# Spreading inverse key norms over a head's rows: products into PSUM or transfers on chip

## The chip, the cores and the metric

The kernel runs on one core of one Trainium2 chip. The time is the device time of one execution in microseconds (us). The engines are TensorE (PE, with its weight loads as PEld), VectorE (DVE), ScalarE (ACT), GpSimd (POOL) and SyncE (SP), which here issues all transfers.

## What is computed

A "macaron" block on 2048 tokens of 128 features: half a step of a six-layer local-attention network, a linear-attention block, and half a step of the same six-layer network again. Everything is float32. The twelve local-attention layers take nearly all of the time. One of them, cut to what matters:

```python
qkv = shift_tokens(x) @ Wqkv                 # 16 heads of 64
q = l2norm(q) * qs ; k = l2norm(k) * ksc     # norm over a head's 64 features
q = q*cos*scale + rotate_half(q)*sin*scale   # rotary, with a growing scale
k = k*cos/scale + rotate_half(k)*sin/scale
sim = 8 * (q . k)  over the own window of 32 tokens and the one before, masked
out = softmax(sim) @ v ; x = out @ Wo + x
x = ffn(shift_tokens(x)) + x                 # layer norm, gated GELU, 341 wide
```

Rotary turns a head's two halves of 32 features into each other and keeps tokens apart, so the inverse norm of a key, one number for each head and token, can be multiplied onto the rotated key.

## The kernel before

Activations lie with features on the 128 partitions and tokens along the free dimension. A layer goes through 8 chunks of 256 tokens; a chunk goes through 4 steps. In a chunk, queries and keys are made in two halves of eight heads (`g2` = 0, 1). In the tile `d["k", g2]` (named abk in the profile, 128 x 2 x 2 x 256) the 128 partitions are 4 groups of 32 feature rows, each group belonging to one head; `i` (0 or 1) picks which four of the eight heads, and `u` which half of a head's features.

The steps that matter, in the order in which data passes through them:

- `project` (L286): TensorE products into PSUM tiles p. VectorE multiplies p with the rotary tables (prod, L295), GpSimd adds the two products (abq and abk, L301). ScalarE squares p (L307), GpSimd adds the two halves of the squares (L321).
- `square_sums` (L329): TensorE sums the squares over each head's rows into the PSUM tile ss. Rows 64 to 127 of ss hold the keys' sums: row 64 + 32i + 4 g2 + j is head j of the four with `i` in half `g2`.
- `norms` (L400 to L408): VectorE and ScalarE make the inverse norms rn (128 rows x 256 tokens, float32) from ss.
- `query_norms` (L416, L422) takes the queries' inverse norms to the scale of the softmax.
- `scale_keys` (L430, L436): the step that changes. Two TensorE products with the 0/1 matrix `sel_r` spread the four rows of rn over their heads' 32 feature rows each, into two PSUM tiles r. VectorE multiplies each onto its half of abk. Then `gather` (L393) issues four transfers that put the keys head by head into hk.
- `earlier_keys` (L450, L451) fills hk's first 32 columns from the chunk before. `similarities` (L466, L476, L488, L489), `exponentials` (L501), `normalised` (L511, L513), `transposed` (L526, L532), `values` (L553, L560, L562) and `output` (L569, L578) are the attention, one step of eight heads and 128 tokens at a time. `values_windows` (L365 to L368) issues the transfers of the value windows vw, `gather` with "q" (L387) those of the queries hq.
- `feed_forward` (L603, L609, L614, L622), for 512 tokens, is spread over the steps of two chunks.

All transfers go through SyncE's one queue, in the order in which they are issued. PSUM has a ring of five tiles ("small") which nearly every TensorE step takes from in turn, two tiles for the scores and one for ss.

The order of all work is written out by hand: the table POS gives each step of each function (a generator, cut at its `yield`) a place (step, position) relative to its chunk. The plan is sorted by step and position, and each engine carries out its own instructions in that order. Before, the first half's `scale_keys` has both parts at (-3, 69) and (-3, 70), the second half's at (-1, 119) and (-1, 136), and the three parts of `norms` are at (-4, 38), (-4, 43) and (-4, 63).

Of the kernel before, what the change touches and what calls it, by code (L numbers as in the profile page):

```python
# [8 lines left out]
F32 = mybir.dt.float32  # L9
BF16 = mybir.dt.bfloat16  # L10
AF = mybir.ActivationFunctionType
ALU = mybir.AluOpType
# [3 lines left out]
P = 128  # L16
# [6 lines left out]
CH = 512  # L23
NCH = N // CH
AC = 256
# [5 lines left out]
HID = 512  # L31
LN_EPS = 1e-5
POS = {
    "tabq": [(-10, 141)],
    "tabk": [(-9, 110)],
    "ss": [(-7, 142)],
    "vwin": [(1, 8)],
    "gq0": [(-5, 13)],
    "gq1": [(-3, 49)],
    "e0": [(0, 76)],  # L40
    "e1": [(0, 77)],
    "nrm": [(1, 10)],
    "qn": [(-2, 106)],
    "ek": [(-1, 73)],
    "proj": [(-9, 135), (-8, 33), (-8, 36), (-8, 37), (-8, 39), (-8, 101)],
    "vproj": [(-2, 24), (-2, 71)],
    "norms": [(-4, 38), (-4, 43), (-4, 63)],
    "sk0": [(-3, 69), (-3, 70)],
    "sk1": [(-1, 119), (-1, 136)],
    "te": [(2, 46), (2, 47)],  # L50
    "av": [(2, 132), (2, 177), (2, 178)],
    "out": [(4, 92), (4, 115)],
    "sim": [(0, 50), (0, 53), (0, 54)],
    "ff": [(11, 99), (12, 30), (12, 130), (13, 21), (13, 94), (14, 139), (15, 124), (15, 149),
        (16, 12), (17, 87), (17, 122), (18, 14), (18, 45), (18, 52), (18, 184), (21, 107),
        (21, 167)],
    "ff2": [(12, 15), (12, 80), (13, 95), (14, 58), (14, 60), (14, 79), (15, 91), (16, 40),
        (16, 58), (16, 147), (16, 182), (16, 187), (16, 191), (17, 34), (17, 111), (17, 121),
        (17, 157)],
    "ff3": [(10, 171), (10, 172), (10, 174), (10, 181), (10, 183), (10, 184), (11, 25), (11, 35),  # L60
        (11, 57), (11, 68), (11, 86), (11, 100), (11, 103), (11, 104), (11, 146), (11, 170),
        (11, 170)],
    "start0": [(-16, 180), (-14, 143), (-13, 66), (-11, 67), (-10, 109), (-10, 185)],
    "start1": [(-10, 65), (-9, 134), (-8, 96), (-8, 148), (-6, 20), (-6, 26)],
    "start2": [(-7, 2), (-7, 117), (-6, 6), (-6, 48), (-4, 74), (-4, 176)],
    "start3": [(-6, 28), (-4, 32), (-4, 44), (-4, 75), (-4, 98), (-4, 188)],
    "sums0": [(-9, 105), (-8, 5), (-8, 88), (-8, 123), (-8, 134), (-7, 102), (-7, 118), (-6, 27)],
    "sums1": [(-1, 137), (-1, 145), (0, 56), (0, 114), (1, 116), (1, 133), (2, 154), (2, 172)],
    "sums2": [(1, 189), (2, 173), (2, 178), (2, 192), (3, 144), (3, 153), (4, 125), (4, 126)],
    "sums3": [(3, 179), (4, 11), (4, 19), (4, 42), (4, 82), (4, 83), (4, 84), (4, 128)],  # L70
    "kv": [(5, 1)],
    "outs0": [(5, 3), (5, 4), (5, 7), (5, 9), (5, 22), (5, 85), (6, 18), (6, 113), (6, 164),
        (7, 17), (7, 90), (7, 129), (7, 163), (7, 190)],
    "outs1": [(6, 61), (11, 78), (12, 131), (13, 120), (13, 127), (13, 140), (13, 160), (14, 59),
        (14, 186), (15, 29), (15, 41), (15, 112), (15, 138), (15, 165)],
    "outs2": [(5, 23), (13, 51), (13, 62), (13, 169), (14, 31), (14, 55), (14, 166), (14, 168),
        (15, 44), (15, 64), (15, 159), (16, 150), (16, 158), (17, 97)],
    "outs3": [(5, 175), (15, 93), (16, 16), (16, 81), (16, 151), (16, 160), (16, 161), (17, 72),
        (17, 89), (17, 108), (17, 152), (17, 156), (17, 162), (18, 155)],
}  # L80
EXP_LN = "natural_log_exp_and_others"

# [11 lines left out]
def kernel(ctx: ExitStack, tc: tile.TileContext, a: dict, out: bass.AP):  # L94
    nc = tc.nc

    const = ctx.enter_context(tc.tile_pool(name="const", bufs=1))
    work = ctx.enter_context(tc.tile_pool(name="work", bufs=2))
# [4 lines left out]
    def small(name):  # L103
        return ps_small.tile([P, CH], F32, tag="small", name=name)

    def keep(shape, name, dtype=F32, src=None):
        t = const.tile(shape, dtype, name=name)
        if src is not None:
            dims = "abc"[: len(shape) - 1]
            flat = t.rearrange(f"p {' '.join(dims)} -> p ({' '.join(dims)})") if len(dims) > 1 else t  # L110
            if dtype == F32:
                nc.sync.dma_start(flat, src)
            else:
                nc.sync.dma_start(t, src)
        return t

    def load_qk(l, g):
        w = const.tile([P, 4, P], F32, tag=f"wqk{g}", name=f"wqk{g}_{l}")
        nc.sync.dma_start(
            w,  # L120
            a["Wqk"][l % DEPTH].rearrange("p (g f) -> p g f", g=4)[:, g, :]
            .rearrange("p (u f) -> p u f", u=4),
        )
        return w
# [25 lines left out]
    def load_x(f):  # L150
        nc.sync.dma_start(xo[:, f * CH : (f + 1) * CH], a["xT"][:, f * CH : (f + 1) * CH])

    load_x(0)
    sq_consts = keep([P, 5, P], "sq_consts", src=a["squares"].rearrange("p a b -> p (a b)"))
    ident, hmask, rot_m = (sq_consts[:, i, :] for i in range(3))
    sel_r = sq_consts[:, 3:5, :]
    wqk = [load_qk(0, g) for g in range(4)]
    rot = keep([P, 2, 2, AC], "rot", src=a["rot"])
    qks = keep([P, DEPTH, 2, 2], "qks", src=a["qks"])
# [108 lines left out]
    def chunk(l, c):  # L268
        return chunks.setdefault((l, c), {"nm": f"{l}_{c}"})
# [154 lines left out]

    def scale_keys(l, c, g2):
        d = chunk(l, c)
        rs = [small(f"r_{d['nm']}_{2 * g2 + i}") for i in range(2)]
        for i in range(2):
            rows = slice(64 + 32 * i, 96 + 32 * i)
            nc.tensor.matmul(  # L430
                rs[i][:, 0:AC], sel_r[rows, g2, :], d["rn"][rows, :], start=True, stop=True
            )
        yield
        for i in range(2):
            k = d["k", g2][:, :, i, :]
            nc.vector.tensor_tensor(  # L436
                k, k, rs[i][:, 0:AC].unsqueeze(1).to_broadcast([P, 2, AC]), ALU.mult
            )
        gather(l, c, "k", g2)

    def earlier_keys(l, c):
# [392 lines left out]
def _shape_constants():  # L834

    import ml_dtypes
    import numpy as np

    freqs = np.arange(0, DH, 2, dtype=np.float64)
    inv = 1.0 / 10000.0 ** (freqs / DH)  # L840
    base = (freqs + 0.4 * DH) / (1.4 * DH)
    t = np.arange(AC, dtype=np.float64)[None, :]
    ang = inv[:, None] * t

    scale = base[:, None] ** ((t - AC // 2) / (WIN // 2))
    cos, sin = np.cos(ang), np.sin(ang)
    rot = np.stack(
        [
            np.stack([8.0 * cos * scale, 8.0 * sin * scale], 1),
            np.stack([cos / scale, sin / scale], 1),  # L850
        ],
        1,
    )

    rot *= 2.0**9
    rot = np.tile(rot.reshape(32, -1), (4, 1)).astype(np.float32)

    back = base ** (AC / (WIN // 2))
    c, s = np.diag(back * np.cos(AC * inv)), np.diag(back * np.sin(AC * inv))
    one = np.block([[c, -s], [s, c]]).reshape(2, 32, 2, 32).transpose(1, 0, 3, 2).reshape(64, 64)  # L860
    rot_m = np.kron(np.eye(2), one)


    i, j = np.arange(WIN)[:, None], np.arange(SK)[None, :]
    near = (j >= i) & (j <= i + WIN)
    off = np.stack([~near, near & (j < WIN)], 1)
    band = np.zeros((2, 2 * WIN, 2, SK), np.float32)
    band[:, :WIN] = np.where(off, -(2.0**100), 0.0)
    band = band.reshape(P, 2, SK).astype(ml_dtypes.bfloat16)
    ident_b = np.tile(np.eye(2 * WIN, WIN), (2, 1)).astype(ml_dtypes.bfloat16)  # L870
    r = np.arange(P)
    sel_r = [r[:, None] % 32 == 4 * i + r[None, :] // 32 for i in range(2)]
    squares = np.stack(
        [r[:, None] == r[None, :], r[:, None] // 8 == r[None, :] // 8, rot_m, *sel_r], 1
    ).astype(np.float32)

    sel = np.zeros((P, 3, 32), np.float32)
    for i in range(2):
        sel[r, i, 4 * i + r // 32] = 2.0**18
    for h in range(HEADS):  # L880
        sel[32 * (h // 2 % 2) + 4 * (h // 8) + 2 * (h // 4 % 2) + h % 2, 2, h] = 1.0
    return {
        "rot": rot,
        "band": band,
        "ident_b": ident_b,
        "squares": squares,
        "sel": sel,
    }


def _laid_out(i):

    import numpy as np

    g = {k: np.asarray(v) for k, v in i.items()}
    a = _shape_constants()
    a["xT"] = g["L0_attn_x"][0].T
    w = g["L0_ffn_Wqkv"]
# [47 lines left out]
```

## Time and profile before

| | |
|---|---|
| median of 3 runs | 3537.21 us (3536.9 to 3539.05) |
| profiled execution | 3536.21 us, of which the profile's span is 3534.4 us |
| mean granted TensorE clock | 0.981 |
| TensorE busy | 3392.8 us (96%) |
| VectorE busy | 2553.6 us (72%) |
| ScalarE busy | 2738.4 us (77%) |
| GpSimd busy | 2092.2 us (59%) |
| L430 on TensorE (r) | 768 records, 145.1 us, mean 429 ns |
| L436 on VectorE (keys times r) | 384 instructions, 246.7 us, mean 684 ns |
| transfers | 396.13 MB, mean 112 GB/s |

A busy time is the union of an engine's instructions. Lines such as L436 are lines of the kernel's file, with the tile written, an arrow and the tiles read. A float32 product on TensorE shows as several records. In a list of idle times, the name behind the arrow is what ended the wait.

### The profile page before, as it was taken

How to read it: one execution, taken by the hardware profiler on the slowest of the kernel's cores; microseconds unless marked ns; L12 is line 12 of the kernel's file. 1: busy time of each engine (PE TensorE's matmuls, PEld its weight loads, DVE VectorE, ACT ScalarE, POOL GpSimd, SP SyncE). 2: the span in 40 equal slices, each digit the busy share in tenths (PEclk: the TensorE clock that was granted, in tenths of full speed). 3: DMA queues.
4: the chain of work that ended last, by engine and by line, in shares of the span. 5: the costliest groups of instructions: out<-in, count | busy, mean ns of one | idle time of the engine just before them, and what ended most of it. 6: DMA issues, size and time to landing. Idle time of an engine off the chain costs nothing.

```text
span 3534.4 us, 154488 instructions
## 1 busy us (share of the span) xinstructions
PE 3392.8 (96%) x64856; PEld 2346.8 (66%) x64856; DVE 2553.6 (72%) x5116; ACT 2738.4 (77%) x8805; POOL 2092.2 (59%) x2195
## 2 busy tenths in 40 slices
PE   7999999999999999999678999999999999999998
PEld 4776776666776677666335777767667666776674
DVE  5777777777777777775336777777777777777774
ACT  4788788878878878887446787888788788788877
POOL 6766666666666566563136666666666666666661
PEclk9999999999999999999788999999999999999999
DMA  4554544444545455444003544545545454544552
GB/s 123 127 127 119 118 120 117 117 122 120 124 115 126 115 122 131 107 115 104 12 12 83 125 123 123 119 114 126 120 122 120 112 127 119 118 121 117 117 123 61
DMA packets 295921, 396.13 MB, mean 112 GB/s; under 512 B 45501, under 2 KB 160953, under 8 KB 295225
## 3 DMA queue, kind: packets, MB, share of 16 engines
q1 hardware_dynamic: 295224, 386.25, 45.3%
q8 instruction: 510, 8.36, 1.0%
q14 instruction: 187, 1.52, 0.1%
HBM read 34.27 MB, written 1.05 MB: 10 GB/s over the span
## 4 chain that ended last, share of the span: by engine, by line
PE 35%; ACT 8%; DVE 6%; issue 1%; POOL 0%; DMA 0%; ACTq 0%; SPq 0%; POOLq 0%; DVEq 0%
PE p L286 7%; ACT e L501 5%; PE av L553 4%; PE y L569 4%; PE pv L345 4%; DVE prod L295 3%; PE sim L476 3%; PE pf L603 2%; PE yf L622 2%; PE te L526 2%; ACT L607 1%; PE r L430 1%; PE ss L329 1%; PE sim L466 1%; DVE eT L532 1%
## 5 line engine op out<-in xcount | busy, mean ns | idle before, releaser
L501 ACT ACTIVATE e<-sim,st,rq 128x64 f32<-128x64 f32 x3072 | 1194.5, 410 | 292.3 <-DVE st L489 288.9
L295 DVE TENSOR_TENSOR prod<-p,tab 128x1024 f32<-128x1024 f32 x768 | 922.3, 1212 | 130.9 <-ACT sq L307 96.1
L513 POOL TENSOR_TENSOR e<-e,st 128x512 f32<-128x512 f32 x384 | 400.5, 1043 | 724.9 <-DVE st L511 697.6
L286 PE MATMUL p<-xa,wqk 128*128 128x256 f32 x3072 | 773.5, 395 | 18.3 <-ACT sq L307 6.3
L301 POOL TENSOR_TENSOR abq<-prod 128x512 f32<-128x512 f32 x384 | 490.2, 1276 | 297.5 <-DVE prod L295 252.9
L501 ACT ACTIVATION_READ_ACCUMULATOR e<-sim,st,rq 128x1 f32 x3072 | 647.9, 211 | 0.0
L307 ACT ACTIVATE sq<-p 128x512 f32<-128x512 f32 x768 | 438.8, 602 | 248.0 <-PE ss L329 101.4
L286 PEld LDWEIGHTS p<-xa,wqk 128*128 128x128 f32 x3072 | 558.2, 191 | 106.5 <-ACT sq L307 9.6
L301 POOL TENSOR_TENSOR abk<-prod 128x512 f32<-128x512 f32 x384 | 487.2, 1269 | 166.6 <-DVE prod L295 89.5
L321 POOL TENSOR_TENSOR sq<-sq 128x256 f32<-128x256 f32 x768 | 546.9, 734 | 0.0
L553 PEld LDWEIGHTS av<-eT,vw 64*64 64x64 f32 x18432 | 401.7, 135 | 171.3 <-DVE st L489 48.0
L553 PE MATMUL av<-eT,vw 64*64 64x32 f32 x18432 | 446.8, 221 | 3.4 <-issue 1.1
L345 PE MATMUL pv<-wv,xa 128*128 128x512 f32 x768 | 413.4, 620 | 19.4 <-ACT gate L609 18.7
L569 PE MATMUL y<-oT,wo 128*128 128x128 f32 x3072 | 395.1, 282 | 0.2 <-DVE oT L562 0.2
L553 PE MATMUL av<-eT,v 64*64 64x32 f32 x6144 | 390.9, 219 | 0.0
L569 PEld LDWEIGHTS y<-oT,wo 128*128 128x128 f32 x3072 | 359.0, 192 | 19.4 <-issue 1.7
L488 DVE TENSOR_REDUCE sim<-sim 128x4 f32<-128x256 f32 x768 | 325.4, 424 | 14.1 <-PE sim L476 14.0
L476 PE MATMUL sim<-hk,hq 64*32 64x64 f32 x24576 | 332.9, 222 | 0.0
L526 PEld LDWEIGHTS te<-sq_consts,e 128*128 128x128 f32 x1536 | 188.5, 141 | 209.4 <-issue 151.6
L553 PEld LDWEIGHTS av<-eT,v 64*64 64x64 f32 x6144 | 325.6, 135 | 0.0
L476 PEld LDWEIGHTS sim<-hk,hq 64*32 64x32 f32 x24576 | 305.6, 105 | 0.2
L603 PE MATMUL pf<-xc,w 128*128 128x512 f32 (+1 forms) x576 | 290.4, 629 | 11.9 <-POOL xc L591 7.5
(141 smaller groups left out, 4549.6 us busy)
## 6 DMA issues: line engine op xcount, KB each, us to landing
hq<-abq SPq DMA_DIRECT2D x384, 256.0 KB
hk<-abk SPq DMA_DIRECT2D x768, 128.0 KB
vw<-v SPq DMA_DIRECT2D x768, 128.0 KB
vw<-v SPq DMA_DIRECT2D x744, 64.0 KB
wqk<-in_Wqk SPq DMA_DIRECT2D x48, 256.0 KB
wv<-in_Wv SPq DMA_DIRECT2D x24, 256.0 KB
wo<-in_Wo SPq DMA_DIRECT2D x12, 512.0 KB
w<-in_W SPq DMA_DIRECT2D x12, 341.0 KB
```

The costliest lines, as they stand in the source:

```text
L286: nc.tensor.matmul(both[s][:, u, :], wqk[g][:, 2 * s + u, :], xs, start=True, stop=True)
L295: nc.vector.tensor_tensor(prod, both[s].unsqueeze(2).to_broadcast([P, 2, 2, AC]), tabs[l, s].rearrange("p (u v) t -> p u v t", u=2), ALU.mult,
L301: nc.gpsimd.tensor_tensor(d["qk"[s], g // 2][:, :, g % 2, :], prod[:, 0], prod[:, 1], ALU.add)
L307: nc.scalar.activation(sq, both[s], AF.Square)
L321: nc.gpsimd.tensor_tensor(sq[:, 0, :], sq[:, 0, :], sq[:, 1, :], ALU.add)
L345: nc.tensor.matmul(ps, xa[:, ti * P : (ti + 1) * P], wv[j], start=True, stop=True)
L476: nc.tensor.matmul(sims[par][WIN * b : WIN * b + WIN, i, :], d["hq"][rows, 4 * h8 + i, at : at + WIN], d["hk"][rows, 4 * h8 + i, at : at + ...
L501: nc.scalar.activation(e[:, i, par, :], d["sims", step][par][:, i, :], AF.Exp, bias=st8[:, 0, i, par : par + 1], scale=rq[:, i, par : par ...
L513: nc.gpsimd.tensor_tensor(ef, ef, st8[:, 1].rearrange("p i r -> p (i r)").unsqueeze(2).to_broadcast([P, 8, SK]), ALU.mult,)
L553: nc.tensor.matmul(av[u][r : r + 64, m, WIN * b : WIN * b + WIN], d["vs", t][u][b][:, at : at + DH], d["eT", step][64 * u : 64 * u + 64, i ...
L569: nc.tensor.matmul(y[:, 0:P], wo[:, i, :], d["oT", t].rearrange("p h u m q -> p (h u m) q")[:, i, :], start=(i == 0), stop=(i == 7),)
L603: nc.tensor.matmul(ps[s][:r], w1[:, s, j * P : j * P + r], x, start=True, stop=True)
```

## The change

`scale_keys` no longer uses TensorE and PSUM. For each half and each `i`, SyncE issues a transfer within SBUF that reads the four rows of rn and writes each of them 32 times, into 128 rows of a new SBUF tile rk (128 x 2 x 256, two buffers). VectorE then multiplies the whole half, both `i`, in one instruction of 1024 elements per partition. The matrix `sel_r` goes, and with it 128 KB of the first load of constants. Then `gather` follows as before.

The table POS is new in nearly all its entries. Those that the text speaks of:

| step | before | after |
|---|---|---|
| norms | (-4, 38), (-4, 43), (-4, 63) | (-4, 37), (-4, 67), (-4, 110) |
| sk0 | (-3, 69), (-3, 70) | (-4, 111), (-3, 73) |
| sk1 | (-1, 119), (-1, 136) | (-4, 141), (-1, 140) |
| vwin | (1, 8) | (1, 62) |
| gq0, gq1 | (-5, 13), (-3, 49) | (-6, 129), (-3, 56) |
| proj, last part | (-8, 101) | (-8, 55) |

```diff
-    sq_consts = keep([P, 5, P], "sq_consts", src=a["squares"].rearrange("p a b -> p (a b)"))
+    sq_consts = keep([P, 3, P], "sq_consts", src=a["squares"].rearrange("p a b -> p (a b)"))
     ident, hmask, rot_m = (sq_consts[:, i, :] for i in range(3))
-    sel_r = sq_consts[:, 3:5, :]
...
     def scale_keys(l, c, g2):
         d = chunk(l, c)
-        rs = [small(f"r_{d['nm']}_{2 * g2 + i}") for i in range(2)]
+        r = work.tile([P, 2, AC], F32, tag="rk", name=f"rk_{d['nm']}_{g2}", bufs=2)
         for i in range(2):
-            rows = slice(64 + 32 * i, 96 + 32 * i)
-            nc.tensor.matmul(
-                rs[i][:, 0:AC], sel_r[rows, g2, :], d["rn"][rows, :], start=True, stop=True
-            )
-        yield
-        for i in range(2):
-            k = d["k", g2][:, :, i, :]
-            nc.vector.tensor_tensor(
-                k, k, rs[i][:, 0:AC].unsqueeze(1).to_broadcast([P, 2, AC]), ALU.mult
-            )
+            row = 64 + 32 * i + 4 * g2
+            nc.sync.dma_start(
+                r[:, i, :],
+                d["rn"][row : row + 4, :].unsqueeze(1).to_broadcast([4, 32, AC]),
+            )
+        yield
+        k = d["k", g2].rearrange("p u i t -> p u (i t)")
+        nc.vector.tensor_tensor(
+            k, k, r.rearrange("p i t -> p (i t)").unsqueeze(1).to_broadcast([P, 2, CH]),
+            ALU.mult,
+        )
         gather(l, c, "k", g2)
```

## The prediction

> **What bounds the kernel now.** I read the page first (busy time by engine, then the slices), then a table by stage of one repeat in the middle of the layers, then the order of events on TensorE, VectorE and SyncE inside that repeat.
>
> ```profile
> span 3534.4 us, 154488 instructions
> ...
> PE 3392.8 (96%) x64856; PEld 2346.8 (66%) x64856; DVE 2553.6 (72%) x5116; ACT 2738.4 (77%) x8805; POOL 2092.2 (59%) x2195
> ...
> q1 hardware_dynamic: 295224, 386.25, 45.3%
> ```
>
> TensorE is busy for 96% of the span; the DMA engines carry 45.3% on one queue. The stage table (length, then busy us of each engine) covers one repeat, two chunks of 256 tokens:
>
> ```profile
> 1000.00:1068.06 68.06, 67.66 (x1366) 47.71 (x1363) 51.94 (x105) 55.42 (x183) 45.17 (x50) 1.00 0.47 118
> ```
>
> Of 68.06 us TensorE is busy 67.66, VectorE 51.94, ScalarE 55.42, GpSimd 45.17, at the full granted clock. The twelve layers are 48 such repeats, 3267 of 3534 us. So what leaves TensorE's order shortens the kernel, as long as the others keep feeding it. In order of time on TensorE, the product that goes:
>
> ```profile
> 1007.24 0.84 PE L476 MATMUL sim<-hk,hq 64*32 64x64 f32 x64
> 1008.01 0.70 PE L430 MATMUL r<-rn,sq_consts 32*128 32x256 f32 x4
> 1008.64 1.99 PE L603 MATMUL pf<-xc,w 128*128 128x512 f32 x4
> ```
>
> From its start to the next group's start it holds TensorE for 1008.64 - 1008.01 = 0.63 us. On VectorE, from the norms (L408) to the product with the keys (L436) and what follows it:
>
> ```profile
> 1003.39 0.42 DVE L408 SCALAR_TENSOR_TENSOR rn<-rn,ss 128x256 f32<-128x256 f32 x1
> ...
> 1009.97 1.28 DVE L436 TENSOR_TENSOR abk<-abk,r 128x512 f32<-128x512 f32 x2
> 1011.93 0.42 DVE L562 COPY oT<-av 128x256 f32<-128x256 f32 x1 [0.67 <-PE av L553]
> 1012.72 0.20 DVE L511 RECIPROCAL st<-st 128x8 f32<-128x8 f32 x1 [0.37 <-ACT e L501]
> 1014.72 0.75 DVE L614 SCALAR_TENSOR_TENSOR h<-pf,lvec,gate 128x512 f32<-128x512 f32 x1 [1.80 <-ACT gate L609]
> ```
>
> In brackets stands VectorE's idle time before the instruction.
>
> **The change, part by part.**
>
> Removed from TensorE: two products for each half chunk, 192 times 0.63 us (12 layers, 8 chunks, 2 halves) = 121 us, all on the bounding engine. With them go four of some 36 PSUM tiles that a chunk takes from the ring of five. TensorE's weight loads sat 42.7 us behind L436 in the chain of waits; I count that at nothing, since TensorE was busy meanwhile.
>
> VectorE's product: before, 384 times 684 ns (L436) = 263 us. After, 192 of 1024 elements. L295, as long, takes 1.21 us; L242, 512 elements with both inputs in SBUF as here, takes at least 0.69. So 1.22 us, 234 us in all. But:
>
> ```profile
> L242 DVE SCALAR_TENSOR_TENSOR xc<-lnt,xc x48: 691/693/1493, 170.6 to 3515.8; 128x512 f32<-128x512 f32 x48
> ```
>
> The slowest of the L242 (1493 ns) began with a GpSimd sum (1.27 us) under way, 0.94 us before its end. So 192 products cost between 234 and 234 + 192 x 1.27 = 478 us: from 29 us less to 215 more, 2.2 us for each chunk of 34. VectorE idles 8 us of each chunk, so I take nothing; the far end is in the range.
>
> Added to SyncE: four issues a chunk, 0.6 us each as hk's are (median 597 ns), 2.4 us of 34 on an engine that sits waiting for L436 for 569 us in all. The first waits for L408; behind it in the queue stand the second half's two, then the query gather and the value windows of the next step. The new order of positions issues them directly behind L408, multiplies the first half 0.8 of a step later and the second three steps later.
>
> The transfers: each reads 4 rows of 1 KB and writes 128 rows of 1 KB. hk's issues also write 128 packets of 1 KB, and land 2.3 us after issue at best, 2.7 in the median (landing events). How long for 4 source rows? No row shows it, so bounds. Lower: as hk, landing within 3.3 us of the norms, both. Upper: the 128 packets one after another, at 46 ns each (fastest tenth of the 1 KB packets) = 5.9 us a transfer. Two rows speak for the upper end. The load of 85 rows of W2 (L144) shows one event 0.53 us after issue and then five, where loads of 128, 64 and 32 rows show sixteen: an engine count that divides the rows, so four for four rows. And a 1 KB packet takes 46 ns while few engines run and 82 to 94 when all sixteen read their 64 neighbouring rows: readers of the same rows slow each other. Four engines on four adjacent rows taking turns are back at one packet each 46 ns.
>
> The Trainium skill speaks against this change twice. "DMA: Bandwidth & Descriptors" (Why a DMA increments its semaphore by 16 and not by 1) makes the number of engines the largest that divides both slowest dimensions, here four, and the 85-row load agrees with its five. "SBUF — State Buffer" (Door 1: The DMA port swizzle) puts four adjacent partitions on one port with 27.6 GB/s measured; rows 64 and 96 share it too. By that page a transfer takes an estimated 4.75 us in place of 5.9 and the wait below is 5.4 us in place of 7.7.
>
> The wait: the second of the pair is issued 0.65 us after L408, its first bytes land 1.7 us later (the earliest landing events of the window transfers), and two transfers follow each other on the same four engines: 0.65 + 1.7 + 2 x 5.9 = 14.1 us. VectorE's own work from L408 to L436 covers 6.2 to 7.8 us, 6.5 in the median; the list of instructions between is the same in the new order. So VectorE stands for 14.1 - 6.5 = 7.7 us a chunk (lower end: none). Behind that instruction in its queue are the attention copies (L562), the reciprocal (L511), h (L614) and the next rotations, which free PSUM for TensorE.
>
> How much reaches TensorE? At least VectorE's idle before the next copy and reciprocal is absorbed (0.67 + 0.37, 1.0 us); at most all its idle of a chunk, (68.06 - 51.94) / 2 = 8.1 us. I take half of that, 4.0, as much of the idle is itself a wait for TensorE. Loss: 3.7 us a chunk, 96 x 3.7 = 355 us. At the start and behind the middle part the chain to the first scores grows by 14 us in place of 0.6: about 25 us in all.
>
> Sum on the profiled run, 3536.2 us (span 3534.4 and 1.8 around it): 3536 - 121 + 355 + 25 = 3795; the median of the three runs is 1.0 us higher: **3796 us**. With 1.0 us absorbed it is 96 x 6.7 = 643, so about 4084. A second way there: the new transfers hold four engines for 4 x 5.9 = 23.6 us a chunk beside the 45.3% of 34.0 = 15.4 they carry, 39 us, more than a chunk lasts; 96 x 5 = 480 us more is 4017. With nearly all absorbed the loss equals the gain.
>
> **The rivals.**
>
> *The transfers land in time* (faster). They decide by one number: landing within about 6.5 us of L408. With sixteen engines it would be 3.3; with four that don't disturb each other 32 packets x 46 to 87 ns (87 = 45.3% of 16 engines' span over the packets) = 1.5 to 2.8 us each, 5.3 to 7.9 for the pair. For it: the new order puts the multiply as far behind as VectorE's work takes. Against: the two rows above. Then the 121 us come back, less what shows up once TensorE is less full: its groups now run about 2.6 us a repeat over their own fastest tenth, and I give back 10 to 35 us. 3537 - 121 + 20 = 3436, between 3410 and 3495.
>
> *The wait is there, and just pays the gain back* (no change): landing 2 to 4 us late with 1.3 us a chunk reaching TensorE: 96 x 1.3 = 121 us, 3537 within 0.2%. This needs a narrow place between the two.
>
> *VectorE and GpSimd block each other* is no case by itself: 2.2 us a chunk against 8 idle.
>
> **How the numbers follow.** The late transfers have 0.61, landing in time 0.35, the tie 0.04. Those are the chances of slower, faster and same; 0.2% is about what a measurement here can tell from no change. The late case alone runs from 3560 to 4090. The range takes in both signs: 3420 to 4090, leaving out the low end of the fast case and a pile-up of both ways to 4084 in the slow one.
>
> **What the profile after would show.** Right: no L430; in the waits, VectorE's product with the keys behind a DMA of rk, some 96 times 5 to 8 us; landing of rk over 10 us after the issue; TensorE's share down to about 88%; more waits of TensorE for VectorE and for vw. The first-half product stands late and the second does not. Wrong, if rk lands within 6 us: then TensorE stays over 97% of a repeat of about 66 us. Wrong in size, if value windows queue behind rk for long, or if VectorE's idle takes it all.

## The result and the profile after

The change costs 1394 us. The median is 4931.04 us (four runs) against 3537.06 us for the kernel before on the same chip, a ratio of 1.395 (95% interval 1.392 to 1.398): slower, and outside the predicted range on the far side of the likeliest case. The profiled execution took 4928.24 us, its span 4926.4 us.

From the page of the kernel after: the span, the busy times, the granted clock by slice (tenths), the DMA queue, and the chain that ended last by engine and by line.

```profile
span 4926.4 us, 153346 instructions
...
PE 3764.0 (76%) x64088; PEld 2549.7 (52%) x64088; DVE 2609.9 (53%) x4924; ACT 2751.0 (56%) x8805; POOL 2157.8 (44%) x2195
...
PEclk7888888888888888888888888888888888888888
...
q1 hardware_dynamic: 345912, 436.46, 42.4%
...
PE 28%; DMA 25%; SPq 19%; DVE 9%; ACT 9%; POOL 6%; issue 5%; DVEq 0%; POOLq 0%; ACTq 0%
DMA rk<-rn 18%; PE p L285 8%; PE pv L344 4%; SPq L365 4%; ACT e L501 4%; SPq L366 3%; DMA vw<-v 3%; SPq L386 3%; PE av L553 3%; SPq L364 3%; DVE prod L294 3%; DMA hk<-abk 2%; SPq L392 2%; PE ss L328 2%; PE sim L476 2%
```

The chain of before, which the profile follows through half of the span only:

```profile
PE 35%; ACT 8%; DVE 6%; issue 1%; POOL 0%; DMA 0%; ACTq 0%; SPq 0%; POOLq 0%; DVEq 0%
```

There, DMA and SyncE's issuing (SPq) stood at 0%. Now they are 44% of a longer span, some 2170 us, and the new transfers (rk from rn) are its largest single line. VectorE, ScalarE and GpSimd are busy about as long as before. TensorE has 768 records fewer and is busy *longer*: 3764 against 3392.8 us, because its granted clock fell from 0.981 to 0.857 in the mean. The queue's share of the 16 engines together did not even rise (45.3% before). So TensorE, VectorE, ScalarE, GpSimd and the DMA engines taken together have time left; the kernel waits.

The stage table of one repeat (length, then busy us of PE, PEld, DVE, ACT, POOL, clock, DMA share, GB/s):

```profile
2603.53:2700.50 96.97, 64.21 (x1230) 47.39 (x1229) 46.71 (x90) 45.29 (x177) 40.34 (x40) 0.81 0.43 88
```

97.0 us in place of 68.06, so 48.5 us a chunk in place of 34.0; a loss of 14.5 us in each of 96 chunks makes 1392 us, the whole result. Where it goes shows in the queues. First VectorE around the norms (L407 now) and the product with the keys (L435); in brackets the idle time before and what ended it:

```profile
2602.45 0.42 DVE L407 SCALAR_TENSOR_TENSOR rn<-rn,ss 128x256 f32<-128x256 f32 x1
...
2615.75 1.22 DVE L435 TENSOR_TENSOR abk<-abk,rk 128x1024 f32<-128x1024 f32 x1 [7.36 <-DMA rk<-rn]
...
2632.60 0.43 DVE L562 COPY oT<-av 128x256 f32<-128x256 f32 x1 [11.53 <-PE av L553]
```

Then SyncE's own queue in the same stretch (start, how long the issuing took, what was issued, how many):

```profile
2602.89 9.09 SPq L429 DMA_DIRECT2D rk<-rn  x4
2612.09 7.25 SPq L386 DMA_DIRECT2D hq<-abq  x2
2619.43 3.79 SPq L365 DMA_DIRECT2D vw<-v  x1
2623.27 2.50 SPq L366 DMA_DIRECT2D vw<-v  x1
```

And GpSimd and TensorE:

```profile
2628.14 1.26 POOL L300 TENSOR_TENSOR abq<-prod 128x512 f32<-128x512 f32 x1 [9.87 <-DMA hq<-abq]
2628.58 0.39 PE L553 MATMUL av<-eT,vw 64*64 64x32 f32 x2 [14.85 <-DMA vw<-v]
```

Read these together. The four new issues, which take 0.6 us each when nothing is in the way, hold SyncE for 9.1 us. VectorE stands 7.36 us for the first pair, as forecast. But the query gather (hq) and the value windows (vw) can be issued only behind them, slowly, and part of their bytes sits behind the new ones: each such transfer leaves sixteen landing events, and of the first hq, issued at 2612.09, twelve come by 2617.88 and the last four from 2625.60 to 2627.28. The second hq is complete at 2627.98 and lets GpSimd go on at 2628.14; vw lets TensorE go on at 2628.58, after 14.85 us. VectorE then waits for TensorE. So two waits follow each other in this chunk; which of them makes the loss is a question for the experiments.

The waits in sum (engine, line, what for: us, times, longest):

```profile
POOL abk L300 <- DMA hk<-abk: 874.0, 154, 7.7
POOL abq L300 <- DMA hq<-abq: 715.1, 84, 16.6
DVE oT L562 <- PE av L553: 676.7, 186, 11.6
DVE abk L435 <- DMA rk<-rn: 605.5, 96, 10.0
ACT v L348 <- DMA vw<-v: 573.2, 84, 10.8
```

Only the fourth is the wait that the change writes into the code, 6.3 us a chunk. The others are for transfers that the change does not touch, or for TensorE's av, which waits for vw. The first two rows of before:

```profile
POOL abk L301 <- DMA hk<-abk: 43.5, 27, 4.1
POOL abq L301 <- DMA hq<-abq: 29.6, 21, 2.9
```

Summed over the span, SyncE's DMA issues took 1829 us before and 3765 us after.

### The profile page after: what moved, and what is told of

Same layout as the page of the kernel before. It is cut to its first block, busy times and chain, and to the rows that moved or that the text cites. A ratio compares the mean times of both kernels' runs of the same rounds, so it can differ in the third digit from the quotient of the medians.

```text
span 4926.4 us, 153346 instructions
## 1 busy us (share of the span) xinstructions
PE 3764.0 (76%) x64088; PEld 2549.7 (52%) x64088; DVE 2609.9 (53%) x4924; ACT 2751.0 (56%) x8805; POOL 2157.8 (44%) x2195
## 4 chain that ended last, share of the span: by engine, by line
PE 28%; DMA 25%; SPq 19%; DVE 9%; ACT 9%; POOL 6%; issue 5%; DVEq 0%; POOLq 0%; ACTq 0%
DMA rk<-rn 18%; PE p L285 8%; PE pv L344 4%; SPq L365 4%; ACT e L501 4%; SPq L366 3%; DMA vw<-v 3%; SPq L386 3%; PE av L553 3%; SPq L364 3%; DVE prod L294 3%; DMA hk<-abk 2%; SPq L392 2%; PE ss L328 2%; PE sim L476 2%
## 5 line engine op out<-in xcount | busy, mean ns | idle before, releaser
L285 PE MATMUL p<-xa,wqk 128*128 128x256 f32 x3072 | 1013.6, 480 | 479.2 <-DVE oT L562 258.4
L285 PEld LDWEIGHTS p<-xa,wqk 128*128 128x128 f32 x3072 | 682.0, 236 | 645.4 <-DVE oT L562 278.8
L300 POOL TENSOR_TENSOR abk<-prod 128x512 f32<-128x512 f32 x384 | 523.8, 1364 | 1037.8 <-DMA hk<-abk 874.0
L553 PE MATMUL av<-eT,vw 64*64 64x32 f32 x18432 | 528.7, 234 | 462.3 <-ACT v L348 280.3
L553 PEld LDWEIGHTS av<-eT,vw 64*64 64x64 f32 x18432 | 469.2, 149 | 667.8 <-ACT v L348 293.3
L435 DVE TENSOR_TENSOR abk<-abk,rk 128x1024 f32<-128x1024 f32 x192 | 287.7, 1499 | 609.8 <-DMA rk<-rn 605.5
L348 ACT COPY v<-pv 128x512 f32<-128x512 f32 x384 | 225.1, 586 | 581.5 <-DMA vw<-v 573.2
L562 DVE COPY oT<-av 128x256 f32<-128x256 f32 x384 | 161.3, 420 | 678.4 <-PE av L553 676.7
L344 PE MATMUL pv<-wv,xa 128*128 128x512 f32 x768 | 497.9, 735 | 16.7 <-DVE lnt L232 9.5
L553 PE MATMUL av<-eT,v 64*64 64x32 f32 x6144 | 468.2, 233 | 0.0
L532 DVE COPY eT<-te 128x512 f32<-128x512 f32 x384 | 262.1, 683 | 134.2 <-PE te L526 134.0
```

The costliest lines, as they stand in the source:

```text
L285: nc.tensor.matmul(both[s][:, u, :], wqk[g][:, 2 * s + u, :], xs, start=True, stop=True)
L300: nc.gpsimd.tensor_tensor(d["qk"[s], g // 2][:, :, g % 2, :], prod[:, 0], prod[:, 1], ALU.add)
L344: nc.tensor.matmul(ps, xa[:, ti * P : (ti + 1) * P], wv[j], start=True, stop=True)
L435: nc.vector.tensor_tensor(k, k, r.rearrange("p i t -> p (i t)").unsqueeze(1).to_broadcast([P, 2, CH]), ALU.mult,)
L553: nc.tensor.matmul(av[u][r : r + 64, m, WIN * b : WIN * b + WIN], d["vs", t][u][b][:, at : at + DH], d["eT", step][64 * u : 64 * u + 64, i ...
```

## Experiments

The question at the start: is it the time of the new transfers, and if so is it the number of engines (four) or the four neighbouring rows; or is it the new order of positions; and what is the rest worth? Times are medians; where there is only one run, the text says so. Edits are against the kernel after unless another one is named.

**Which rows are read.** Two versions have the same transfers in bytes and packets. In the first, the 0/1 matrix `sel` of the square sums writes each head's sum four times, so that sixteen neighbouring rows of rn hold the four heads' norms; in the second, there are four rows as before, but eight apart. (The matrix that picks out the queries' norms follows along.)

```diff
-            row = 64 + 32 * i + 4 * g2
+            row = 64 + 32 * i + 16 * g2                                 # e1_sixteen
-    d["rn"][row : row + 4, :].unsqueeze(1).to_broadcast([4, 32, AC])
+    d["rn"][row : row + 16, :].unsqueeze(1).to_broadcast([16, 8, AC])
-        sel[r, i, 4 * i + r // 32] = 2.0**18
+        for copy in range(4):
+            sel[r, i, 16 * i + 4 * (r // 32) + copy] = 2.0**18
```

> The same number and size of transfers in the same order, but each reads 16 neighbouring rows (every inverse norm is made in four copies by TensorE's sums of squares) and writes each 8 times. Theory A (four engines reading four neighbouring rows make each transfer 5 us long, and all the rest follows from that): rk lands within 3.5 us of its issue, VectorE no longer waits for it, TensorE is over 96% busy in a repeat of two chunks, 3410 to 3470 us. Theory B (the added issues and packets crowd SyncE's queue, whatever the engines): time stays over 4500 us. Theory C (VectorE's product with two SBUF inputs and GpSimd block each other, or the new order of work is worse): the transfers are fast, yet the time stays well over 3537 us.

```diff
+            row = 64 + 32 * i + g2                                      # e2_four_apart
+    d["rn"][row : row + 25 : 8, :].unsqueeze(1).to_broadcast([4, 32, AC])
+        sel[r, i, 8 * (r // 32) + i] = 2.0**18
```

> Still four source rows for each transfer, but 8 rows apart in place of neighbours. If the four engines slow each other because they read neighbouring rows (theory A1), a 1 KB packet takes about 46 to 90 ns, a transfer 1.5 to 2.9 us, and rk lands 4 to 7 us after the first issue: VectorE waits at most 1 us a chunk and the time falls to 3420 to 3650 us. If the count of four engines is enough by itself (theory A2: one engine needs about 155 ns for a packet of this kind), nothing changes: a landing of 12 us and about 4930 us.

e1: 3614.22 us, ratio 1.023 (1.021 to 1.026). e2: 3633.14 us (one run). Their waits for the new transfers, from the rows on the tile rk, e1 and then e2 (us, times):

```profile
  DMA rk<-rn: 2.6, 2
```

```profile
  DMA rk<-rn: 2.0, 1
```

Later, eight neighbouring rows were tried, halfway between.

```diff
+            row = 64 + 32 * i + 8 * g2                                  # e13_eight
+    d["rn"][row : row + 8, :].unsqueeze(1).to_broadcast([8, 16, AC])
+        for copy in range(2):
+            sel[r, i, 8 * i + 2 * (r // 32) + copy] = 2.0**18
```

> The change with eight neighbouring source rows for each transfer (two copies of every inverse norm, eight engines), same order of work. Theory A (everything follows from how long a transfer holds its engines and the queue): a transfer takes about half of the 5 us of four rows, the fourth lands about 10 us after its issue in place of 18, and since some of that is covered as in the run with rows apart (fourth landing at 6.6 us, 3633 us), the time lies between that and the change, 3750 to 4250 us. If only four rows are special (a fixed fault of that shape): as with 16 rows, 3600 to 3650 us.

3929.86 us (one run). Landing of the new transfers after their own issue, medians by order in the chunk, from the landing events:

| kernel | 1st | 2nd | 3rd | 4th | time |
|---|---|---|---|---|---|
| 4 neighbouring rows (after) | 7.5 | 12.1 | 17.0 | 18.0 | 4931 |
| 8 neighbouring rows (e13) | 4.7 | 6.6 | 8.6 | 8.9 | 3930 |
| 4 rows, 8 apart (e2) | 3.3 | 4.1 | 5.4 | 6.7 | 3633 |

For sixteen neighbouring rows the median over all is 4.2 us (middle four fifths: 3.4 to 5.3). e2 reads four rows, as the kernel after does, but its fourth transfer is in after 6.7 us and not 18. So what is slow is neither four source rows nor the 128 packets as such: it is that the four rows are neighbours. The share of the loss that goes with it: from 4931 to 3633 by e2, 1298 of 1394 us, and 1317 by e1, which has more rows as well. Neither gets below before: theory A of e1 was right that VectorE's wait goes, and wrong about the time. In the kernel after, a quarter of the 1 KB packets took 151 ns or more and a tenth 159 or more, where before nine in ten took at most 94. 32 of them one after another on each of four engines, 32 x 155 ns, are 5.0 us a transfer.

**The transfers without the wait.** Before's kernel, products and all, and the same four transfers a chunk into a tile that nothing reads:

```diff
+    def spread_unused(l, c, g2):                # e4_unused, against before
+        d = chunk(l, c)
+        r = work.tile([P, 2, AC], F32, tag="rk", name=f"rk_{d['nm']}_{g2}", bufs=2)
+        for i in range(2):
+            row = 64 + 32 * i + 4 * g2
+            nc.sync.dma_start(r[:, i, :],
+                d["rn"][row : row + 4, :].unsqueeze(1).to_broadcast([4, 32, AC]))
...
+    "un0": [(-4, 64)], "un1": [(-4, 94)],
```

> The kernel before, with its products into PSUM, and beside them the four transfers of rk for each chunk, into a tile that nobody reads, issued right behind the norms and 30 positions later. If VectorE's wait for rk is all of the loss, this is 3537 to 3600 us. Theory A (the transfers also hold up the issue queue and the four engines for everything behind them, value windows and query gathers): 3900 to 4500 us, with TensorE and ScalarE waiting for vw, and no wait of VectorE for rk.

4772.76 us (one run): 1236 us more than before, though VectorE never waits for rk and TensorE keeps its products. Its waits:

```profile
POOL abq L303 <- DMA hq<-abq: 1522.9, 88, 20.9
DVE oT L574 <- PE av L565: 1152.9, 235, 15.2
ACT v L351 <- DMA vw<-v: 868.1, 81, 14.3
```

The queue alone makes nearly the whole loss, 1236 of 1394 us. The opposite try gives the waiting product more room, one step later, and puts the value windows one step earlier:

```diff
-    "sk0": [(-4, 111), (-3, 73)],
+    "sk0": [(-4, 111), (-2, 73)],               # e12_four_rows_reordered
-    "vwin": [(1, 62)],
+    "vwin": [(0, 62)],
```

> The change as it is, four neighbouring source rows, but the first half's multiplication one step later (at (-2, 73)) and the window transfers before the transfers of rk (at (0, 62)). VectorE's wait for rk (605 us) and the wait of TensorE and ScalarE for vw (about 1000 us together) should nearly go. If those two waits are the loss, the time falls from 4931 to under 4000 us. If the four engines are simply full (20 us of rk a chunk beside what they carry), the waits move to the query gathers and hk and the time stays over 4500 us.

4957.71 us (one run), nothing gained. The longest wait now, and what is left of VectorE's wait for rk (605.5 us in the kernel after):

```profile
POOL abq L300 <- DMA hq<-abq: 1370.8, 94, 17.8
DVE abk L435 <- DMA rk<-rn: 16.7, 17, 2.7
```

The wait that the change writes into the code is gone, but the kernel is no faster. The time moves from one transfer to another, as the second alternative had it, though not for the reason given there: the four engines are not full, as is worked out further down. With one queue, whatever is issued behind rk pays.

**Without transfers: what the removal is worth.** Here the new transfers go and the keys are multiplied by a constant tile, first with the new order of positions, then with before's:

```diff
-        r = work.tile([P, 2, AC], F32, tag="rk", ...)     # e3_no_transfer
-        for i in range(2): ... nc.sync.dma_start(...)
+        k = d["k", g2].rearrange("p u i (s t) -> p (u i s) t", s=2)
+        nc.vector.tensor_tensor(k, k, mean_w.unsqueeze(1).to_broadcast([P, 8, P]), ALU.mult)
...
+POS = before's POS                                        # e6_none_old_plan: this too
```

> No transfers of rk at all: VectorE multiplies the keys by a constant tile in SBUF, in one instruction of 1024 elements with both inputs in SBUF, at the same place; so the inverse key norms are left out. Theory A: all of the loss is the transfers', 3410 to 3450 us, with VectorE's product at 1.2 to 2.5 us. Theory C (lock between VectorE and GpSimd, or the new order): the time stays over 3600 us.

> No transfers of rk and no products: VectorE multiplies the keys by a constant tile, in the order of work of before. The inverse key norms are left out. Theory P: with the old order TensorE's saving shows, 3420 to 3470 us. Theory L (VectorE and GpSimd hold each other up at the product with two SBUF inputs): 3510 to 3570 us, as in the new order.

e3: 3558.97 us (one run). e6: 3519.73 us, ratio 0.996 (0.994 to 0.997). With no transfer to wait for and two TensorE products a half chunk less, e6 gains 0.4% on before, not 121 us, and e3 lies between the two theories' ranges. Two further kernels, both on e6, ask why:

```diff
-        nc.vector.tensor_tensor(k, k, mean_w..., ALU.mult)             # e9_no_product
```

```diff
-        nc.vector.tensor_tensor(k, k, mean_w.unsqueeze(1)..., ALU.mult)
+        k = d["k", g2].rearrange("p u i t -> p (u i) t")               # e10_psum_constant
+        nc.vector.tensor_tensor(k, k, const_ps.unsqueeze(1).to_broadcast([P, 4, AC]), ALU.mult)
```

In e10 the constant lies in one half of ss's PSUM bank, and the intermediate of the norms, which had been there, in SBUF.

> In the order of work of before, without products into PSUM, without transfers of rk and without VectorE's product: the inverse key norms are left out altogether. If TensorE was the bound and VectorE's new product is what ate its 121 us (theory L), this falls to 3400 to 3440 us. If something else that neither part touches holds the pace (theory S, for slack: TensorE's full row in the profile was partly work stretched to fill), it stays at 3490 to 3520 us, close to the 3520 of the run with the product.

> As the run with the constant tile in the old order (3520 us), but the constant lies in PSUM, so VectorE's product has one SBUF input and the same length of 1024 elements; to make room, one intermediate of the norms moves from PSUM to SBUF. The inverse key norms are left out. Theory L1 (the lock between VectorE and GpSimd costs): GpSimd's busy time falls back from 2280 to about 2090 us, the product takes 1.22 us always, 3420 to 3470 us. Theory L2 (the length of the product costs) or S: 3500 to 3530 us.

e9: 3495.3 us, 0.988 (0.986 to 0.990). e10: 3489.15 us, 0.987 (0.986 to 0.989). The multiply itself costs nothing that can be measured (e9 against e10, whose intervals overlap; e10 also has that intermediate in another place), but reading its second operand from SBUF costs e6 - e10, about 31 us. The rows of the multiply, e6 and then e10 (ns shortest/median/longest):

```profile
L428 DVE TENSOR_TENSOR abk<-abk,mean_w x192: 1215/1535/2350, 51.9 to 3451.6; 128x1024 f32<-128x1024 f32 x192
```

```profile
L432 DVE TENSOR_TENSOR abk<-abk,bank x192: 1208/1222/1223, 52.4 to 3423.3; 128x1024 f32<-128x1024 f32 x192
```

With the operand in PSUM all 192 take the same time; with it in SBUF the median is 0.31 us longer and the longest nearly twice as long, and GpSimd's busy time goes from 2101.5 to 2280.1 us. The two engines block each other in both directions. The Trainium skill says so ("SBUF — State Buffer", Who interferes with whom): a VectorE instruction with two SBUF inputs contends with a GpSimd instruction that reads SBUF. These two rows agree.

**What bounds it once the products are gone.** Even e10 keeps only 46 of the 121 us. The waits of TensorE for the feed-forward's gate, which holds the PSUM ring while ScalarE computes it, before and then e9:

```profile
PEld pv L345 <- ACT gate L609: 45.0, 54, 1.0
...
PE pv L345 <- ACT gate L609: 18.7, 51, 0.5
```

```profile
PEld pv L344 <- ACT gate L597: 121.8, 81, 2.2
PE pv L344 <- ACT gate L597: 82.9, 79, 1.8
```

That points at ScalarE as the next limit. To test it, both kernels were made with a gate that needs no change of ScalarE's function table:

```diff
-            nc.scalar.preload_act_table_set("gelu_and_others")
...
-                gate[:r], ps[1][:r], AF.Gelu, bias=...
+                gate[:r], ps[1][:r], AF.Square, bias=...
-            nc.scalar.preload_act_table_set(EXP_LN)
```

> The kernel before with a lighter ScalarE: the gate of the feed-forward in the layers is a square in place of GELU, in the table set that the rest uses, so 288 table loads of 1.28 us go (370 us of ScalarE's 2738). The layers' GELU is left out. If TensorE was the bound (theory T), the time barely moves: 3500 to 3530 us. If ScalarE is close behind and shares the bound (theory S): 3440 to 3490 us.

> The run without products, transfers and multiplication (3495 us), with the same lighter ScalarE: no inverse key norms, and a square in place of the layers' GELU. Theory S (ScalarE's feed-forward gate holds PSUM and with it TensorE, once the products are gone): 3380 to 3430 us, so that TensorE's 121 us come back when ScalarE no longer stands in the way. If neither sets the pace but the fixed order with its chain of short waits does: 3460 to 3495 us.

e14 (before, relieved): 3492.6 us, 0.988 (0.987 to 0.989). e15 (e9, relieved): 3366.37 us, 0.952 (0.950 to 0.954). Their difference is 126 us, where e9 is only 42 us below before. So with ScalarE relieved the removal is worth about what TensorE's rows say. Both differences also contain VectorE's multiplication, which e9 and e15 leave out; what it costs with ScalarE relieved was not measured. The same stretch in e9 and then e15 (columns as in the stage table above):

```profile
2400.00:2536.00 136.00, 131.73 (x2733) 94.56 (x2732) 95.06 (x200) 112.58 (x372) 85.79 (x89) 1.00 0.49 120
```

```profile
2400.00:2536.00 136.00, 135.81 (x2821) 97.24 (x2814) 99.23 (x202) 99.66 (x366) 91.63 (x97) 1.00 0.50 124
```

ScalarE at 112.58 of 136 us is far from full by its share, and it still keeps TensorE from filling up.

**The order of positions.** Before's products under the new table; sixteen rows under before's table; sixteen rows with the value windows back at their old place:

```diff
+    "sk0": [(-3, 72), (-3, 73)], "sk1": [(-1, 139), (-1, 140)],   # e5_plan_alone: before's scale_keys
```

```diff
+POS = before's POS, with                                          # e7_sixteen_old_plan, on e1
+    "sk0": [(-4, 64), (-3, 70)], "sk1": [(-4, 94), (-1, 136)],
```

```diff
-    "vwin": [(1, 62)],
+    "vwin": [(1, 8)],                                             # e8_sixteen_windows8, on e1
```

> The products into PSUM as before, in the new order of work (each pair of products right in front of its multiplications, at the places of the new multiplications). If the new order is what keeps the run without transfers at 3559 us (theory P: eight window transfers now stand in SyncE's queue right in front of the second half's key gather, GpSimd waits for that gather to give abk back, and TensorE waits for GpSimd's sums of squares), this is slower than before, 3570 to 3680 us, with GpSimd waiting several hundred us for hk. If the order is as good as the old one and VectorE's longer product with two SBUF inputs is to blame (theory L), 3520 to 3550 us.

> Transfers of 16 source rows in the order of work of before; they are issued right behind the norms (second half 30 positions later), the multiplications stand where they stood. Theory P: close to the run without transfers in that order plus what the added issues cost, 3430 to 3500 us, faster than before. Theory L: 3540 to 3620 us.

> Transfers of 16 source rows in the new order of work, with one entry put back: the window transfers at (1, 8) as before in place of (1, 62). Theory P (they stand in front of the key gather): GpSimd's wait for hk falls from 570 to under 150 us and the time from 3614 to 3430 to 3520 us. Otherwise it stays at about 3614 us.

e5: 3723.87 us, 1.053 (1.051 to 1.055). e7: 3558.69 us, 1.007 (1.005 to 1.008). e8: 3625.3 us, 1.025 (1.024 to 1.027). The new order costs something in every company: 187 us with the products, some 39 us without transfers (e3 against e6), 59 us with sixteen rows (e1 against e7, by their ratios). It isn't that the window issues now stand in front of the key gather: e8 undoes that and gains nothing (its wait for hk falls only to 435.5 us). What shows is GpSimd waiting for the key gather, which has to read abk before GpSimd may write it again, before and then e1:

```profile
POOL abk L301 <- DMA hk<-abk: 43.5, 27, 4.1
```

```profile
POOL abk L300 <- DMA hk<-abk: 570.4, 132, 7.7
```

In e7 it is 95.4 us. In e3, which has the new order and no new transfer at all, it is 435.6 us, so much of the first row of the kernel after (874.0 us) is the order's and not the burst's. Which entry of the table makes it was not found. e7 itself missed theory P's range: against e6 it is 39 us longer, and GpSimd waits 208.6 us for hq in place of 12.3.

**Versions that might be faster.** On e7: the product on GpSimd; the product as two of 512 elements; and the three gates of a feed-forward taken together, so that ScalarE changes its table twice and not six times (192 loads of 1.28 us fewer). The last also on the kernel before.

```diff
-        nc.vector.tensor_tensor(k, k, r..., ALU.mult)
+        nc.gpsimd.tensor_tensor(k, k, r..., ALU.mult)             # e11_sixteen_gpsimd
```

```diff
+        for i in range(2):                                        # e16_sixteen_split
+            ki = d["k", g2][:, :, i, :]
+            nc.vector.tensor_tensor(ki, ki, r[:, i, :].unsqueeze(1).to_broadcast([P, 2, AC]), ALU.mult)
```

```diff
+        gates = [up(j, 1) for j in range(3)]                      # e17_sixteen_grouped, e18_before_grouped
+        nc.scalar.preload_act_table_set("gelu_and_others")
+        for j, (r, p) in enumerate(gates):
+            nc.scalar.activation(h[:r, j, :], p[:r], AF.Gelu, bias=...)
+        nc.scalar.preload_act_table_set(EXP_LN)
...
+        # then, for each j: h[:r, j] = (up(j, 0) + bias) * h[:r, j]
```

> Transfers of 16 source rows in the old order of work, with the product of keys and norms on GpSimd in place of VectorE, so that VectorE has no product with two SBUF inputs there. By GpSimd's rows (1.27 us for a sum of 512) a product of 1024 is about 2.5 us, 192 of them 490 us, GpSimd 2580 us busy in all, 73% of the span. Theory L1: the lock is gone, and if GpSimd's longer queue is hidden 3430 to 3500 us, faster than before. If GpSimd's order of work is itself the close second bound, 3560 to 3700 us.

> Transfers of 16 source rows in the order of work of before (3559 us), with the multiplication in two instructions of 512 elements as before, so that GpSimd can get in between. If the lock between VectorE and GpSimd is held for the length of an instruction, GpSimd waits less at a time but VectorE has twice as many entries to wait for: 3540 to 3570 us; under 3530 us it would beat the kernel before.

> Transfers of 16 source rows in the order of work of before (3559 us), with the three gates of a feed-forward computed one behind the other, into h itself, so that the table is changed twice for each feed-forward and not six times: 192 loads of 1.28 us less on ScalarE, 246 us. The result is the reference's. Theory S: with ScalarE lighter, TensorE's saving shows: 3430 to 3500 us, faster than before. If the lumped gates hold up the exponentials behind them as much as the loads did: 3530 to 3570 us.

> The kernel before with the same grouped gates. By the run with the lighter gate (3493 us, 288 loads less) two thirds of 44 us: 3500 to 3525 us. Theory S says that the products into PSUM keep this one above the run with transfers of 16 rows and grouped gates; if it is as fast or faster, the exchange of products for transfers isn't worth making even with ScalarE relieved.

| kernel | time | ratio (95%) |
|---|---|---|
| e11, product on GpSimd | 3628.13 | 1.026 (1.025 to 1.028) |
| e16, two products | 3573.07 | 1.010 (1.008 to 1.012) |
| e17, sixteen rows, gates together | 3519.26 | 0.996 (0.994 to 0.997) |
| e18, before with gates together | 3533.36 | 1.000 (0.999 to 1.001) |

e11: on GpSimd the product takes 2.36 us in place of 1.53, and it costs 70 us against e7. e16: two short products are no better than one long one. e17 is the one version that leaves nothing out and is below before, by 0.4%, with its whole interval under 1: with the source rows spread, before's order and ScalarE relieved, the idea of the change pays that much. It was forecast at 3500 us or less. Grouping alone (e18) pays nothing, although e14 gained 44 us by relieving the same gate further. Grouping also holds three PSUM tiles of the ring at once; whether that takes the gain back was not tried.

## Why the prediction was wrong, step by step

The steps from before to after, each by one comparison of ratios, in us of 3537:

| step | by | us |
|---|---|---|
| products gone, operand in PSUM | e10 against before | -46 |
| operand in SBUF | e6 against e10 | +31 |
| transfers that land in time | e7 against e6 | +39 |
| the new order | e1 against e7 | +59 |
| four neighbouring rows for sixteen | after against e1 | +1316 |

**The side and the cause were right.** Of the two readings of the trace, late or in time, the late one came, and for the reason given: four engines on four neighbouring rows slow each other. The landing events of the first two transfers show one event about 1.0 us after the issue and then four. A transfer was put at 5.9 us; the packets give 5.0 us, and from one landing to the next 5.3, 5.6 and 4.9 us pass in the median. The second transfer was in 12.8 us after L407, against 14.1 forecast. VectorE's wait was put at 7.7 us a chunk and measured 6.3, 96 times, as the forecast had it.

One of the two rows behind it does not say what it was taken to say. The prediction has a 1 KB packet take 46 ns while few engines run. In the trace of before, 15 packets of the queue were under way in the median halfway through the 1 KB packets of at most 46 ns, and 15 as well through those of 82 to 95 ns. So the 46 ns are no sign of few engines. A packet of the slow transfers takes 155 ns on each of four engines, one every 39 ns; that one every 46 ns came so close was luck in part. What shows the cause is e2.

The Trainium skill has the rate ("SBUF — State Buffer", Door 1: The DMA port swizzle): four neighbouring partitions share one port, for which it gives 27.6 GB/s. 128 KB in 5.0 us are 26 GB/s, so the measurement agrees, and its 4.75 us was the better estimate of the two. By the same table eight neighbouring rows lie on two ports, sixteen on four, and rows eight apart on one each; the order of the landing times of the four kernels agrees.

**The step that failed is "How much reaches TensorE".** It took 3.7 us a chunk (355 us); the whole loss was 14.5 us a chunk, and 13.7 of them come with the four neighbouring rows alone (after against e1). That step followed VectorE's wait through VectorE's slack, and offered the pile-up on the four engines as *a second way* to a similar number, 4017. They are not two ways to one number, and the pile-up is the one that counts. e4 has it without any wait of VectorE for rk and loses 1236 us, 12.9 us a chunk; in e12 that wait falls from 605.5 to 16.7 us and the total stays.

The pile-up was also priced by the wrong measure, as throughput: 23.6 us of new plus 15.4 us of old traffic is 39 us, five more than a chunk lasts. With the measured 5.0 us it is 20 + 15.4 = 35 us, if the old traffic is spread evenly, and the chunk takes 48.5. The four engines are not full: in the repeat shown (96.97 us), the packet records have no packet of the queue under way for 14.0 us, and only three or four for 39.3 us. In e12 none is under way for 988 us of the span, in the kernel after for 890. It is latency: some 20 us of bytes are queued at once. A transfer spread over all sixteen engines is complete only when its last four shares are, as hq showed above; or it is issued late, as in e4, where hq lands 3.7 us after its own issue, as before, and GpSimd still waits up to 20.9 us for it. The chunk has several such transfers, each in a loop that goes round once a chunk (hq frees abq for GpSimd, hk frees abk, vw feeds TensorE).

A bound that fits is the burst, less a fixed slack of the loops behind it in the queue. Four times the mean time between landings makes the burst 21.0 us in the kernel after, 10.1 in e13 and 7.4 in e2. Against e1 these lose 13.7, 3.3 and 0.2 us a chunk, which leaves a slack of 7.3 and 6.8 us, and of at least some 7.2 in e2, which loses next to nothing. e2 and e13 are one run each, and which loop has this slack is not shown. The prediction's own last line, "Wrong in size, if value windows queue behind rk for long", named the pile-up; it should have been a term of the sum.

**The credit of 121 us was too large.** With nearly everything else as in before (the multiplication takes a constant, and one intermediate of the norms lies elsewhere), e10 gets 46 us. 67.66 us busy of 68.06 read as if nothing else were near the edge, but ScalarE was close behind (e14 and e15). So the rival *The transfers land in time* was wrong in size as well: e1 and e2 meet its condition (landing within about 6.5 us, waits of 2 to 3 us in the whole run) and take 3614 and 3633, e7 3559, where it had 3410 to 3495. Its deduction of 10 to 35 us was for waits of this kind, and too small.

**Smaller terms.** The lock between VectorE and GpSimd was dismissed as no case by itself against 8 us of idle time; it costs 31 us, inside the bounds named for it but not the nothing that was taken, and GpSimd is busy for longer as well (2280.1 against 2101.5 us). The new order was taken as the list of instructions that it makes for VectorE, at no cost; by itself it costs 39 to 187 us. TensorE's share was put at 88% and is 76%, at a lower clock that the prediction did not expect to move.

## What to carry to other kernels

Price a transfer by the rows it *reads*: the same 128 KB took 5 us on its way from four neighbouring rows, and the first of a chunk landed 7.5 us after its issue, but within 3.3 us of its issue from four rows eight apart. When a slow burst enters a shared in-order queue, list every transfer behind it and the loop that each one closes, and price their delay by itself: here it made 1236 of 1394 us without the wait that the code shows. And before crediting work taken from an engine at 96 to 99%, look at what is next: here only 46 of 121 us came, and two kernels with ScalarE relieved showed why.

## What the runs showed of the hardware

Issuing is not a fixed price. The issue of a new transfer took 0.6 us where the queue flowed (e1, e2: 0.61 and 0.62 in the median) and 1.4 us in the median, up to 4.1, in the kernel after; the issues of hq and vw right behind it took 2.5 to 3.9 us each in the chunk shown. As far as these rows show, a queue whose bytes back up stops the engine that feeds it.

TensorE's granted clock was lower in the runs that left TensorE idle for longer: 0.981 at 96% busy before, 0.974 at 92% in e1, 0.947 at 88% in e13, 0.857 at 76% after, 0.835 at 72% in e12. The busy share alone does not set it: e5 has 0.962 at 94%, e9 0.980 at 93%. How much the lower clock adds to the loss was not separated. Its busy time in the kernel after, 3764 us, is for work that took 3257 to 3280 us at 0.98 (e6, e9, e10).
